# Last self attention of a two-layer Perceiver: division after the product, one subtraction on GpSimd, the row sums of W behind the output projection

## The chip, the cores and the metric

The kernel runs on one core of a Trainium2 chip. The metric is the device time of one execution in microseconds (us), as the median of several runs; lower is better. Engines are named as in the profile: PE is TensorE (PEld its weight loads), DVE VectorE, ACT ScalarE, POOL GpSimd, SP the engine that issues the DMAs. All data is 32-bit floating point.

## The reference

128 latent rows of width 256 (`x`) pass through two layers against one context of 12544 rows of width 192. Each layer is a cross attention to the context, a self attention over the 128 rows, and a mixture of 8 experts of which each row uses 2; each of the six steps reads a layer-normalised `x` and is added to `x`. The change lies in the second layer's self attention, and in one product that it needs from W:

```python
def _L1_attn_ref(x, W):                       # x: layer-normalised, [1, 128, 256]
    scale = 1.0 / sqrt(D)                     # D = 256
    scores = einsum('btd,bsd->bts', x, x) * scale
    probs = softmax(scores, axis=-1)
    vacuum_mask = probs < 0.01
    vacuum_energy = where(vacuum_mask, probs, 0.0)
    vac_sum = vacuum_energy.sum(axis=-1, keepdims=True)
    vac_in = broadcast_to(vac_sum, (B, T, D))
    casimir = einsum('btd,od->bto', vac_in, W)
    sparse_probs = where(vacuum_mask, 0.0, probs)
    sparse_probs = sparse_probs / (sparse_probs.sum(axis=-1, keepdims=True) + 1e-09)
    attended = einsum('bts,bsd->btd', sparse_probs, x)
    return attended + casimir * 0.01
```

Since `vac_in` is one number per row, `casimir` is that number times the row sums of W.

## The kernel before

The 128 latents lie on the 128 partitions throughout; `x` is one tile of 128 x 256, and every step makes a new one. The two cross attentions take most of the time.

**Cross attention of the second layer.** 16 heads of width 64 are taken in pairs, eight passes (`PASSES`) of 13 periods (`NS`) over 1024 context rows each, 104 periods (`NP`) in all. A loop over `t` runs the scores of period `t` and, `LAG` = 14 periods later, the product with the values, so its last 14 rounds hold the values and products of the last pass alone. Each such round has TensorE compute the values of one period (L228, L235), ScalarE copy them out of PSUM (L962) and exponentiate a probability tile (L1057), and TensorE multiply the two into the PSUM tile `both` (L1069). VectorE and GpSimd subtract the row maximum (L1051) ahead of that, and VectorE adds up the exponentials (L1092). In the round `t == NP + 3` two products stand that belong to no period: the row sums of W, as a product of a tile of ones with the transposed W (`awT`), into the second half of `both`'s second bank (L1160), and the output projection of the first seven passes (L1138). After the loop come the last denominator (L1124, L1133), the last pass's projection (L1138), the bias row (`add_row`, L126) and the residual `x4` (L162).

**Self attention.** `layernorm` (statistics on VectorE, a square root on ScalarE, L146 on VectorE, two transposes on TensorE at L156 and their copy at L157), then the scores (L1248), their maximum, the exponential on ScalarE (L1254), the sum, the reciprocal and the probabilities `a1_p` (L1261). From there VectorE makes the small probabilities, their sum, the large ones, their sum and its reciprocal, divides, TensorE transposes (L156), VectorE copies (L157), TensorE multiplies with the normalised `x` (L1278), and VectorE adds the residual and the row sums of W times the small probabilities' sum (L1283).

**Experts of the second layer.** `layernorm`, the router's product (L1291), then for each expert 32 products of 128 x 128 into PSUM (L1302), a gate on ScalarE, a multiplication on VectorE (L1313), and four products back to width 256 (L1340). Their weights, 24 transfers of 512 KB, are issued by SP in the order of the program, each as soon as its slot of the ring of 28 tiles is free; the same slots hold the probability tiles of the cross attention.

**What sets the order.** The code around the change stands under a manual schedule: each engine executes its instructions in the order of the program, and waits on semaphores between engines are put in by the framework. PSUM tiles of 512 elements (`ps_mm`, `ps_t`, `ps_w` are one kind) come from a pool of four buffers. [...]In the profile's names leading letters of a tile are cut (`a1_p` is `a_p`), and `xn` of the self attention is `ln` on its own or `ln4`.

Of the kernel before, what the change touches and what calls it, by code (L numbers as in the profile page):

```python
# [8 lines left out]
F32 = mybir.dt.float32  # L9
AF = mybir.ActivationFunctionType  # L10
ALU = mybir.AluOpType
AX = mybir.AxisListType

P = 128
D = 256
# [18 lines left out]
def perceiver(ctx: ExitStack, tc: tile.TileContext, a: dict, out: bass.AP):  # L34
    nc = tc.nc
# [31 lines left out]
    ps_wide, ps_t, ps_mm = ps_s, ps_w, ps_w  # L67
# [81 lines left out]
    def transposed(pool, t, n, name, tag, bank=None, **kw):  # L149

        tT = pool.tile([P, n, P], F32, tag=tag, name=name, **kw)
        for g in range(0, n, 4):
            m = min(4, n - g)
            pt = ps_t(f"{name}_ps{g}") if bank is None else bank
            for i in range(m):
                nc.tensor.transpose(pt[:, i * P : (i + 1) * P], t[:, (g + i) * P : (g + i + 1) * P], ident)  # L156
            nc.vector.tensor_copy(tT[:, g : g + m, :].rearrange("p c n -> p (c n)"), pt[:, : m * P])  # L157
        return tT
# [736 lines left out]
    with tc.tile_pool(name="l1x", bufs=1) as work:  # L895
# [246 lines left out]
        with tc.manual_schedule():  # L1142
            for t in range(NP + LAG):
                before, live = t - LAG, t < NP
                e = before + 1
                end = live and periods[t][1] == NS - 1
                if before == NP - 1:
                    pass_end(PASSES - 1)
                o = attend(before) if 0 <= before else None
                if 0 < t <= NP and periods[t - 1][1] == NS - 1:  # L1150
                    pass_spread(periods[t - 1][0])
                if t == NP + 1:
                    context(t)
                    ywo.extend(
                        slot_weight(f"ywo{i}", a["L1_xattn_Wo"][512 * i : 512 * i + 512]) for i in range(2)
                    )
                if t == NP + 3:

                    for c in range(2):
                        nc.tensor.matmul(  # L1160
                            final["both"][:, 1, D : 2 * D], ones, awT[:, c, :], start=(c == 0), stop=(c == 1)
                        )
                    projected(0, PASSES - 1)
                if t != NP + 1 and (NS <= t + 1 < NP or 0 <= e + 1 < NP):
                    context(t)
                k = keys(t + 1) if NS <= t + 1 < NP else None
                if t < NS:
                    kTs[t] = firstk[t]
                v = values(e + 1) if 0 <= e + 1 < NP else None
                sts = scores(t) if live else None  # L1170
                if v:
                    if k:
                        k[0]()
                    v[0]()
                if 0 <= e < NP and periods[e][1] == 0:
                    shifted(e)
                if 0 <= e + 1 < NP and periods[e + 1][1]:
                    shifted(e + 1)
                late = 0 <= e < NP and periods[e][1] < 2
                if 0 <= e < NP and not late:  # L1180
                    exponents(e)
                    if e == NP - 1:
                        table(AF.Sqrt, "ln4_table0")
                if o is not None:
                    added(before, 0)
                    if not end:
                        added(before, 1)
                    attended(before, o)

                short = k and v and periods[t + 1][1] == NS - 1  # L1190

                def evicted():
                    k[2](1)
                    for r in range(2):
                        v[2](r)

                if short:
                    for f in (k, v):
                        for r in range(2):
                            f[1](r)  # L1200
                if live:
                    keep(t, sts, evicted if short else None)
                if t < NS:
                    fill(2 if t < 4 else 1)
                if t in (5, 7):
                    queries(*((1, 5) if t == 5 else (5, 8)))
                if end:
                    fold(periods[t][0])
                if late:
                    exponents(e)  # L1210
                if short:
                    k[2](0)
                elif k and v:
                    for r in range(2):
                        k[1](r)
                    for r in range(2):
                        k[2](r)
                final_v = v and t == NP - 1
                if final_v:
                    for f in v[1:]:  # L1220
                        for r in range(2):
                            f(r)
                if end:
                    pass_maximum(periods[t][0])
                if o is not None:
                    if end:
                        added(before, 1)
                    del ps[before]
                if v and not short and not final_v:
                    for r in range(2):  # L1230
                        v[1](r)
                    for r in range(2):
                        v[2](r)
                if 0 < before and periods[before - 1][1] == NS - 1:
                    pass_end(periods[before - 1][0])
            nc.vector.tensor_tensor(oT[:, PASSES - 1, :], final["both"][:, 0, 0:P], os[PASSES - 1], ALU.mult)
            projected(PASSES - 1, PASSES)
            py = final["both"][:, 1]
            add_row(py[:, :D], ROW_BO, D)
            x = residual(x, py[:, :D], "x4")  # L1240
            wsum = final["both"][:, 1, D : 2 * D]


    with tc.tile_pool(name="l1a", bufs=1) as work, tc.manual_schedule():
        xn, xnT = layernorm(x, "ln4")
        ps = ps_mm("a1_ps")
        for c in range(2):
            nc.tensor.matmul(ps[:, :P], xnT[:, c, :], xnT[:, c, :], start=(c == 0), stop=(c == 1))  # L1248
        nmax = small.tile([P, 1], F32, tag="s_nmax", name="a1_nmax")
        nc.vector.tensor_reduce(nmax, ps[:, :P], AX.X, ALU.max, negate=True)  # L1250
        nb = small.tile([P, 1], F32, tag="s_nb", name="a1_nb")
        nc.vector.tensor_scalar(nb, nmax, 1.0 / 16.0, None, ALU.mult)
        ex = work.tile([P, P], F32, name="a1_e")
        nc.scalar.activation(ex, ps[:, :P], AF.Exp, bias=nb, scale=1.0 / 16.0)  # L1254
        table(AF.Sqrt, "ln5_table0")
        tot = small.tile([P, 1], F32, tag="s_tot", name="a1_tot")
        nc.vector.tensor_reduce(tot, ex, AX.X, ALU.add)
        rtot = small.tile([P, 1], F32, tag="s_rtot", name="a1_rtot")
        nc.vector.reciprocal(rtot, tot)
        pr = work.tile([P, P], F32, name="a1_p")  # L1260
        nc.vector.tensor_scalar(pr, ex, rtot, None, ALU.mult)  # L1261
        vac = work.tile([P, P], F32, name="a1_vac")
        nc.vector.scalar_tensor_tensor(vac, pr, 0.01, pr, ALU.is_lt, ALU.mult)
        vs = small.tile([P, 1], F32, tag="s_vs", name="a1_vs")
        nc.vector.tensor_reduce(vs, vac, AX.X, ALU.add)
        sp = work.tile([P, P], F32, name="a1_sp")
        nc.vector.tensor_tensor(sp, pr, vac, ALU.subtract)
        ss = small.tile([P, 1], F32, tag="s_ss", name="a1_ss")
        nc.vector.tensor_reduce(ss, sp, AX.X, ALU.add)
        ss1 = small.tile([P, 1], F32, tag="s_ss1", name="a1_ss1")  # L1270
        nc.vector.tensor_scalar(ss1, ss, 1e-9, None, ALU.add)
        rs = small.tile([P, 1], F32, tag="s_rs", name="a1_rs")
        nc.vector.reciprocal(rs, ss1)
        spn = work.tile([P, P], F32, name="a1_spn")
        nc.vector.tensor_scalar(spn, sp, rs, None, ALU.mult)
        spT = transposed(work, spn, 1, "a1_spT", tag="spT")
        pa = ps_mm("a1_pa")
        nc.tensor.matmul(pa[:, :D], spT[:, 0, :], xn, start=True, stop=True)  # L1278
        x = residual(x, pa[:, :D], "x5a")
        vs1 = small.tile([P, 1], F32, tag="s_vs1", name="a1_vs1")  # L1280
        nc.vector.tensor_scalar(vs1, vs, 0.01, None, ALU.mult)
        y = xp.tile([P, D], F32, tag="x", name="x5")
        nc.vector.scalar_tensor_tensor(y, wsum, vs1, x, ALU.mult, ALU.add)  # L1283
        x = y


    with tc.tile_pool(name="l1f", bufs=2) as work, tc.manual_schedule():
# [108 lines left out]
```

## Time and profile before

| | |
|---|---|
| median of 3 runs | 1573.84 us (1573.14 to 1574.27) |
| the profiled execution | 1575.52 us |
| its span, first to last instruction | 1573.8 us |
| PE busy | 1498.2 us, 95% |
| DVE busy | 1153.5 us, 73% |
| ACT busy | 997.9 us, 63% |
| POOL busy | 873.4 us, 55% |
| mean granted TensorE clock | 0.991 |
| chain that ended last, by engine | PE 65%, DVE 7%, ACT 4% |
| row sums of W (L1160) | 1459.6 to 1460.6 us |
| end of the cross attention, last residual | about 1511 us |
| self attention, layer norm included | about 1511 to 1522.3 us |
| router and experts | about 1522.3 us to the end |

A row of a timeline has the start in us from the span's start, the duration in us, the engine, the line, the operation, what it writes `<-` what it reads, the sizes, and the number of instructions merged; in brackets stands how long the engine was idle before and what ended that. A row of a table of stretches has the busy time in us and the number of instructions of PE, PEld, DVE, ACT and POOL, then the granted TensorE clock as a share of full speed, the share of time in which the DMA engines were busy, and GB/s. A 32-bit matrix product appears as two records per instruction.

### The profile page before, as it was taken

Reading aid. Unit: us, or ns where it says so; the run is one execution under the profiler, and the core shown is the slowest. Engines: PE = TensorE matmul, PEld = TensorE weight load, DVE = VectorE, ACT = ScalarE, POOL = GpSimd, SP = SyncE. Lnnn points to the kernel's source line nnn. Section 1 sums busy time; section 2 is a strip of 40 time slices with the busy share of each in tenths; the row PEclk is TensorE's granted clock in tenths of the full one; section 3 lists DMA queues with packets and bytes.
Section 4 is the critical chain, followed back from the end, with each engine's and each line's share of the span. In section 5 each row is a group of like instructions: output and inputs, shape, how many; then the busy total and the mean of one; then the engine's idle time right before and its main releaser. Section 6 shows DMA issues by size and latency. Waiting matters only on the chain.

```text
span 1573.8 us, 39767 instructions
## 1 busy us (share of the span) xinstructions
PE 1498.2 (95%) x17138; PEld 1151.3 (73%) x17138; DVE 1153.5 (73%) x1219; ACT 997.9 (63%) x1233; POOL 873.4 (55%) x570
## 2 busy tenths in 40 slices
PE   7999989999879999999999999999999999999979
PEld 4666656666545877787787787787787787788968
DVE  3899887999884337777777777777777777778742
ACT  4898988999883235665565565565565665666541
POOL 0488877988840000864864864864764764764400
PEclk9999999999999999999999999999999999999979
DMA  3111021211086861222222222232232232234680
GB/s 105 44 60 42 27 62 42 62 42 42 14 246 189 264 168 29 82 82 86 82 83 85 81 86 82 81 93 75 84 97 70 86 95 73 90 88 131 176 293 4
DMA packets 68737, 146.62 MB, mean 93 GB/s; under 512 B 8905, under 2 KB 27089, under 8 KB 68562
## 3 DMA queue, kind: packets, MB, share of 16 engines
q1 hardware_dynamic: 68258, 143.30, 30.7%
q8 instruction: 135, 2.21, 0.6%
q10 hardware_dynamic: 304, 0.79, 0.2%
q14 instruction: 40, 0.33, 0.1%
HBM read 143.92 MB, written 0.13 MB: 92 GB/s over the span
## 4 chain that ended last, share of the span: by engine, by line
PE 65%; DVE 7%; ACT 4%; issue 1%; DMA 1%; POOL 1%; DVEq 0%; ACTq 0%
PE x_s L977 11%; PE x_v L235 11%; PE x_k L213 10%; PE x_o L1069 10%; PE x_v L228 6%; PE x_k L210 4%; PE f_h L1302 2%; PE f_h L839 2%; PE f_py L856 2%; DVE x_part L1096 2%; PE x_both L1069 1%; ACT x_p L522 1%; PE k L213 1%; DVE x_folded L1024 1%; POOL x_p L511 1%
## 5 line engine op out<-in xcount | busy, mean ns | idle before, releaser
L1051 POOL TENSOR_TENSOR x_p<-x_p,x_spread 128x1024 f32<-128x1024 f32 (+1 forms) x186 | 427.5, 2325 | 151.4 <-ACT x_spread L1042 151.1
L511 POOL TENSOR_TENSOR x_p<-x_p,x_spread 128x512 f32<-128x512 f32 (+1 forms) x184 | 324.4, 1809 | 127.1 <-ACT x_spread L499 65.3
L1096 DVE TENSOR_REDUCE x_part<-x_p 128x256 f32<-128x1024 f32 (+1 forms) x175 | 329.6, 1923 | 0.0
L994 ACT COPY x_p<-x_s 128x1024 f32<-128x1024 f32 (+1 forms) x200 | 197.9, 996 | 179.4 <-DVE x_mx L1001 97.6
L1001 DVE TENSOR_TENSOR x_mx<-x_s,x_mx 128x1024 f32<-128x1024 f32 (+1 forms) x161 | 193.4, 1201 | 128.7 <-PE x_s L977 120.2
L1101 POOL TENSOR_TENSOR x_sums<-x_sums,x_part 128x256 f32<-128x256 f32 x161 | 117.6, 731 | 299.8 <-DVE x_part L1096 297.9
L446 ACT COPY x_p<-x_s 128x1024 f32<-128x1024 f32 x196 | 193.3, 1015 | 50.8 <-PE x_s L433 35.5
L235 PEld LDWEIGHTS x_v<-ywv_lo,x_ctx_lo 128*128 128x128 f32 x1568 | 189.3, 192 | 38.4 <-issue 36.8
L1057 ACT ACTIVATE x_p<-x_p 128x1024 f32<-128x1024 f32 (+1 forms) x200 | 197.9, 1037 | 2.2 <-DVE x_p L1051 2.0
L522 ACT ACTIVATE x_p<-x_p 128x1024 f32<-128x1024 f32 x196 | 196.5, 1063 | 0.2 <-DVE x_p L511 0.2
L235 PE MATMUL x_v<-ywv_lo,x_ctx_lo 128*128 128x128 f32 x1568 | 193.2, 276 | 0.0
L452 DVE TENSOR_TENSOR x_mx<-x_s,x_mx 128x1024 f32<-128x1024 f32 x140 | 168.1, 1220 | 32.7 <-PE x_s L433 17.8
L977 PE MATMUL x_s<-x_qT,x_kT 64*128 64x128 f32 x2744 | 177.7, 279 | 0.0
L977 PEld LDWEIGHTS x_s<-x_qT,x_kT 64*128 64x128 f32 x2744 | 160.2, 188 | 15.6 <-issue 15.4
L213 PE MATMUL x_k<-x_ctx_lo,ywk_lo 128*128 128x512 f32 (+1 forms) x364 | 171.6, 594 | 0.0
L1069 PE MATMUL x_o<-x_p,x_v 128*64 128x128 f32 x2744 | 169.6, 276 | 0.4
L962 ACT COPY x_v<-x_v 128x512 f32<-128x512 f32 (+1 forms) x208 | 116.4, 563 | 77.2 <-PE x_v L235 76.5
L1069 PEld LDWEIGHTS x_o<-x_p,x_v 128*64 128x64 f32 x2744 | 148.4, 137 | 11.0 <-issue 1.7
L228 PEld LDWEIGHTS x_v<-ywv_hi,x_ctx_hi 64*128 64x128 f32 x1568 | 105.5, 188 | 46.7 <-issue 25.4
L433 PE MATMUL x_s<-x_qz,x_kT 32*128 32x256 f32 x1568 | 118.6, 403 | 17.7 <-ACT x_p L446 16.6
L535 PE MATMUL x_o<-x_p,x_v 128*32 128x128 f32 x3136 | 113.0, 278 | 10.4 <-ACT x_p L522 7.6
L535 PEld LDWEIGHTS x_o<-x_p,x_v 128*32 128x32 f32 x3136 | 82.8, 111 | 54.5 <-ACT x_p L522 18.2
(268 smaller groups left out, 1774.0 us busy)
## 6 DMA issues: line engine op xcount, KB each, us to landing
x_ctx_lo<-in_ctxT_dram SPq DMA_DIRECT2D x119, 512.0 KB, 4.1
x_ctx_hi<-in_ctxT_dram SPq DMA_DIRECT2D x238, 128.0 KB, 4.0
f_w<-in_L_ffn_W_dram SPq DMA_DIRECT2D x32, 512.0 KB, 4.9
k_lo<-in_ctxT_dram SPq DMA_DIRECT2D x12, 512.0 KB, 8.3
f_gating<-n_kernel_gating_EDF_dram SPq DMA_DIRECT2D x8, 512.0 KB, 10.6
f_up<-L_ffn_kernel_up_EDF_dram SPq DMA_DIRECT2D x8, 512.0 KB, 10.4
f_wd<-ffn_kernel_down_EFD_dram SPq DMA_DIRECT2D x8, 512.0 KB, 10.3
k_hi<-in_ctxT_dram SPq DMA_DIRECT2D x24, 128.0 KB, 7.6
```

Source lines behind the costliest of these rows:

```text
L213: nc.tensor.matmul(ps[r][:, :h], wk[0][:, js], lo[:, r * h : (r + 1) * h], start=False, stop=True)
L228: nc.tensor.matmul(ps[r][:, ks], hi[rs, ks], wv[1][rs, js], start=(kc == 0), stop=False, skip_group_check=True,)
L235: nc.tensor.matmul(ps[r][:, kc * P : (kc + 1) * P], lo[:, r * h + kc * P : r * h + (kc + 1) * P], wv[0][:, js], start=False, stop=True, sk ...
L511: engine.tensor_tensor(v, v, by[:, banks].unsqueeze(2).to_broadcast([P, n, 2, 256]), ALU.add)
L522: nc.scalar.activation(ps[t][k], ps[t][k], AF.Exp)
L535: nc.tensor.matmul(os[b][32 * i : 32 * i + 32, u * P : (u + 1) * P], v[:, 2 * g + c, 17 * (2 * i + u) : 17 * (2 * i + u) + 32], p[i // 2][ ...
L977: nc.tensor.matmul(st[:, u, c * P : (c + 1) * P], kTs[t][rs, ks], qT[rs, j, :], start=True, stop=True)
L994: nc.scalar.copy(scores_kept(ps[t][i], sts[i].shape[2] // P), sts[i])
L1051: engine.tensor_tensor(v, v, by.unsqueeze(2).to_broadcast([P, 2, n, P]), ALU.add)
L1057: nc.scalar.activation(v, v, AF.Exp)
L1069: nc.tensor.matmul(o[us, 0:P], vs[t][:, c0 + c, us], p[:, n0 : n0 + P], start=(c0 + c == 0 and (s == 0 or not whole)), stop=(c0 + c == tot ...
L1096: nc.vector.tensor_reduce(part, v, AX.X, ALU.add)
```

## The change

- The row sums of W (two products of 128 x 256) leave the round `t == NP + 3`. They now stand after the residual `x4` in the program, behind the bias row in TensorE's order, with a PSUM tile of their own (`a1_pc`).
- The large probabilities are made straight from the probabilities, by one instruction with the comparison turned round, and not by subtraction.
- Their transpose follows at once, without the division; the sum, the guard and the reciprocal stand between the transpose and its copy in VectorE's order. The transpose is written out in place of the helper.
- The small probabilities are now the difference of the two, computed on GpSimd after the product with `xn` is issued; VectorE sums them after the copy.
- The residual takes the row sums' term first (L1281 of the changed kernel), then the product times the reciprocal (L1283), both as one multiply-and-add instruction. Formerly it was one addition and one multiply-and-add.

VectorE has two instructions less, GpSimd one more, TensorE as many as before.

```diff
                 if t == NP + 3:
-                    for c in range(2):
-                        nc.tensor.matmul(
-                            final["both"][:, 1, D : 2 * D], ones, awT[:, c, :], start=(c == 0), stop=(c == 1)
-                        )
                     projected(0, PASSES - 1)
...
             x = residual(x, py[:, :D], "x4")
-            wsum = final["both"][:, 1, D : 2 * D]
+            pc = ps_mm("a1_pc")
+            for c in range(2):
+                nc.tensor.matmul(pc[:, :D], ones, awT[:, c, :], start=(c == 0), stop=(c == 1))
...
         nc.vector.tensor_scalar(pr, ex, rtot, None, ALU.mult)
-        vac = work.tile([P, P], F32, name="a1_vac")
-        nc.vector.scalar_tensor_tensor(vac, pr, 0.01, pr, ALU.is_lt, ALU.mult)
-        vs = small.tile([P, 1], F32, tag="s_vs", name="a1_vs")
-        nc.vector.tensor_reduce(vs, vac, AX.X, ALU.add)
         sp = work.tile([P, P], F32, name="a1_sp")
-        nc.vector.tensor_tensor(sp, pr, vac, ALU.subtract)
+        nc.vector.scalar_tensor_tensor(sp, pr, 0.01, pr, ALU.is_ge, ALU.mult)
+        pt = ps_t("a1_spT_ps")
+        nc.tensor.transpose(pt[:, 0:P], sp, ident)
         ss = small.tile([P, 1], F32, tag="s_ss", name="a1_ss")
         nc.vector.tensor_reduce(ss, sp, AX.X, ALU.add)
         ss1 = small.tile([P, 1], F32, tag="s_ss1", name="a1_ss1")
         nc.vector.tensor_scalar(ss1, ss, 1e-9, None, ALU.add)
         rs = small.tile([P, 1], F32, tag="s_rs", name="a1_rs")
         nc.vector.reciprocal(rs, ss1)
-        spn = work.tile([P, P], F32, name="a1_spn")
-        nc.vector.tensor_scalar(spn, sp, rs, None, ALU.mult)
-        spT = transposed(work, spn, 1, "a1_spT", tag="spT")
+        spT = work.tile([P, P], F32, name="a1_spT")
+        nc.vector.tensor_copy(spT, pt[:, 0:P])
         pa = ps_mm("a1_pa")
-        nc.tensor.matmul(pa[:, :D], spT[:, 0, :], xn, start=True, stop=True)
-        x = residual(x, pa[:, :D], "x5a")
+        nc.tensor.matmul(pa[:, :D], spT, xn, start=True, stop=True)
+        vac = work.tile([P, P], F32, name="a1_vac")
+        nc.gpsimd.tensor_tensor(vac, pr, sp, ALU.subtract)
+        vs = small.tile([P, 1], F32, tag="s_vs", name="a1_vs")
+        nc.vector.tensor_reduce(vs, vac, AX.X, ALU.add)
         vs1 = small.tile([P, 1], F32, tag="s_vs1", name="a1_vs1")
         nc.vector.tensor_scalar(vs1, vs, 0.01, None, ALU.mult)
-        y = xp.tile([P, D], F32, tag="x", name="x5")
-        nc.vector.scalar_tensor_tensor(y, wsum, vs1, x, ALU.mult, ALU.add)
-        x = y
+        y = xp.tile([P, D], F32, tag="x", name="x5a")
+        nc.vector.scalar_tensor_tensor(y, pc[:, :D], vs1, x, ALU.mult, ALU.add)
+        x = xp.tile([P, D], F32, tag="x", name="x5")
+        nc.vector.scalar_tensor_tensor(x, pa[:, :D], rs, y, ALU.mult, ALU.add)
```

## The prediction, made before the changed kernel ran

> **What bounds the kernel now.** I read the page's slices first. TensorE is nearly full everywhere except in the last slices but one, and there its granted clock falls:
>
> ```profile
> PE   7999989999879999999999999999999999999979
> PEclk9999999999999999999999999999999999999979
> ```
>
> The chain of waits is 65% TensorE. In order of time it lies on TensorE alone up to 1507.9 us and again from 1525.4 us. The change touches both sides of that first border. So the second view is TensorE's timeline around 1460 us, where the row-sum product stands (L1160):
>
> ```profile
> 1457.72 1.97 PE L1069 MATMUL x_both<-x_p,x_v 128*64 128x128 f32 x32
> 1459.62 1.13 PE L1160 MATMUL x_both<-awT,ones 128*128 128x256 f32 x4
> 1460.58 3.19 PE L1138 MATMUL x_both<-ywo,x_oT 128*128 128x256 f32 x14
> ```
>
> No idle time stands before these groups, and the waits of TensorE between 1458 and 1510 us hold one entry, 1.0 us before the last projection. The four records of L1160 are paid in full.
>
> The third view is VectorE's timeline through the attention (start, duration, in brackets the idle time before):
>
> ```profile
> 1516.91 0.29 DVE L1261 TENSOR_SCALAR a_p<-a_e,a_rtot 128x128 f32<-128x128 f32 x1
> 1517.23 0.29 DVE L1263 SCALAR_TENSOR_TENSOR a_vac<-a_p 128x128 f32<-128x128 f32 x1
> 1517.56 0.29 DVE L1265 TENSOR_REDUCE a_vs<-a_vac 128x1 f32<-128x128 f32 x1
> 1517.76 0.28 DVE L1267 TENSOR_TENSOR a_sp<-a_p,a_vac 128x128 f32<-128x128 f32 x1
> 1518.08 0.29 DVE L1269 TENSOR_REDUCE a_ss<-a_sp 128x1 f32<-128x128 f32 x1
> 1518.40 0.15 DVE L1271 TENSOR_SCALAR a_ss<-a_ss 128x1 f32<-128x1 f32 x1
> 1518.58 0.16 DVE L1273 RECIPROCAL a_rs<-a_ss 128x1 f32<-128x1 f32 x1
> 1518.78 0.28 DVE L1275 TENSOR_SCALAR a_spn<-a_sp,a_rs 128x128 f32<-128x128 f32 x1
> 1519.70 0.29 DVE L157 COPY a_spT<-a_spT_ps 128x128 f32<-128x128 f32 x1 [0.63 <-PE a_spT_ps L156]
> 1521.30 0.42 DVE L162 TENSOR_TENSOR x5a<-a_pa,x 128x256 f32<-128x256 f32 x1 [1.31 <-PE a_pa L1278]
> 1521.64 0.14 DVE L1281 TENSOR_SCALAR a_vs<-a_vs 128x1 f32<-128x1 f32 x1
> 1521.83 0.48 DVE L1283 SCALAR_TENSOR_TENSOR x<-x_both,a_vs,x5a 128x256 f32<-128x256 f32 x1
> ```
>
> Everything here is serial: TensorE waits for VectorE and the reverse, and nothing else fills the time. What this chain loses, the end gains. The chain puts 8.5 us before L1257 down to a weight DMA (f_up). I don't believe it: that transfer belongs to the expert layer, behind this layer in the program, and ScalarE's a_e ended 0.09 us before L1257 began.
>
> The fourth view is a table of stretches, cut at the steps of the granted clock (PE busy is the second number, the clock the third from the right):
>
> ```profile
> 1505.90:1509.31 3.41, 2.39 (x45) 2.15 (x41) 1.25 (x2) 1.03 (x2) 0.00 (x0) 1.00 1.06 372
> 1509.31:1512.72 3.41, 1.27 (x4) 0.54 (x4) 1.61 (x5) 0.94 (x2) 0.00 (x0) 1.00 1.06 377
> 1512.72:1516.14 3.42, 1.89 (x6) 1.22 (x6) 0.87 (x3) 1.05 (x3) 0.00 (x0) 0.50 1.06 373
> ```
>
> The clock halves at 1512.72 and is whole again at 1529.79, five stretches of 3.41 us later.
>
> **Part 1: the row sums leave the full stage.** L1160 starts at 1459.62 and L1138 at 1460.58: at most 0.96 us. From 1459.62 to the next group (L228 at 1463.70) 18 records take 4.08 us, 0.227 each, so four are 0.91; four weight loads alone (0.19 each) give 0.76. I take 0.91, with 0.76 and 0.96 as ends. It reaches the end if nothing else is late in that stage. ScalarE idles 1.65 us per period there waiting for x_v of TensorE itself; GpSimd's last spread ends at 1472.4, for tiles used later; the context loads are issued several periods ahead of use and land in about 4 us; the last sums (x_allsums, ends 1505.80) are 0.5 us ahead of x_den, and follow TensorE through ScalarE. SP's expert loads follow the freed slots and move with it; the last lands near 1526, the first expert needs its own, issued at 1490, only after 1522. None is next.
>
> **Part 2: the row sums behind the projection.** The same two products (four records) now stand behind add_row (L126, last starts at 1510.2, done 1510.6) and ahead of the transposes of ln4 (1512.85), which wait for VectorE, ScalarE and VectorE. At 0.227 each they need 0.91 us, at half clock, as a_pa (1.22 for two records), 2.4 us at most; the gap is 2.27. So 0, at worst 0.2. The residual x4 waits for add_row alone.
>
> **Part 3: a shorter chain.** Before, from a_vac's start (1517.23) to the start of the last x (1521.83) it is 4.60 us. After:
> - a_sp is one instruction of a_vac's form, from a_p: 0.29. As from a_spn's start to its transpose (1518.78 to 1519.22), 0.44; I take 0.45.
> - transpose start to copy start 0.48 (1519.22 to 1519.70), copy to a_pa 0.35 (1520.05), a_pa to the next VectorE start 1.25 (1521.30).
> - Sum 2.53, so the last x starts at 1519.76, and lasts 0.48 as before: 2.07 us saved.
>
> The sum over a_sp, the guard and the reciprocal (a_ss, ss1, rs) take the 0.62 us in which VectorE formerly idled for the transpose: rs starts at 1518.06, and the copy's turn is 1518.16, just when its transpose is ready. Worth 0 (up to 0.1 late).
>
> **Part 4: GpSimd's subtraction.** a_vac moves to GpSimd, which has nothing behind it, but VectorE's reduction a_vs waits for it, and behind that in VectorE's queue are vs1, x5a and the last x. Its price: GpSimd's forms are 2367 ns at 1024 elements, 1271 at 512, 731 at 256, about 2.1 ns an element over 0.19 us, so an estimate of 0.46 us at 128. In the timeline GpSimd starts 0.14 us after VectorE's x_part (1444.27 to 1444.41). Its instruction carries twelve waits; ScalarE's a_e, with eleven, began 0.16 us after VectorE instead of the usual 0.04, so 0.12 more. a_sp ends at 1517.52, a_vac at 1518.24, ahead of VectorE's turn after the copy (1518.36). Then a_vs 0.33, vs1 0.18, x5a 0.50 with their gaps: done 1519.37, 0.39 before a_pa is ready. Cost 0; if it came later than 0.4 us, each further us costs one. Not below 0, for nothing waits for it earlier.
>
> [...]By the rows this operation has run hundreds of times in the program, and starts 0.14 us after its releaser even after 5 us of idleness, though here it has idled 45 us.[...]
>
> **Part 5: the clock.** [...]In the table above the window before the drop was 37% busy, not idle; elsewhere one of 64% busy (430.71 to 434.12) kept its clock. [...]With this run's grid, the transposes of ln4 move 0.91 us forward into the full-clock window: 0.44 (x_mt, L246) instead of 0.66, 0.22 gained. Then f_pl starts 3.2 us earlier, at 1522.2, and the next full busy window ends at 1526.38, so 4.2 us of TensorE work at half clock instead of 4.4: 0.1. On another grid a_ps too runs at full clock (another 0.6), or the warm-up falls a window later (up to 1.2 lost). I take 0.25.
>
> **Sum.** 0.91 + 0 + 2.07 + 0 + 0.25 = 3.23 us. The profiled execution took 1575.5 us for a span of 1573.8, and would take 1572.3. It lies 1.7 us above the median of the runs; the difference carries over: 1573.84 - 3.23 = 1570.6.
>
> **Rivals.**
> - The row sums' 0.91 us is taken by another wait in the full stage (x_v copies, context loads): 1571.5. Against it: no such idle time in TensorE's rows.
> - GpSimd is late by more than its slack without a stall (rows of GpSimd are rough, and twelve waits were never seen on it), by 0.5 to 1.5 us: 1571.1 to 1572.1. For it: a cross-engine trip on a path with 0.4 us of slack.
> [...]- The transpose is moved but the chain isn't cut, since the copy waits for VectorE's three small steps or the product for a PSUM bank: at most 0.6 us lost, 1571.2. Against it: the product waits only for the copy.
>
> **Chances.** A difference of 0.2% (3.15 us, below 1570.7 or above 1577.0) is about what a measurement of this kernel can tell. As summed, 1569.4 to 1571.6 by the grid: 0.72, of which 0.49 below 1570.7. Another wait takes the row sums: 0.11 (0.02 below, by the grid). GpSimd late by up to 1.5: 0.10. The 6 us: 0.03, of which 0.02 beyond 1577. Chain not cut: 0.04 (0.01 below). Faster 0.52, within 0.46, slower 0.02. The range runs from the lower end of the grid, 1569.4, to the late GpSimd, 1572.3; it leaves out the 6 us and the tails.
>
> **What would show it.** L1138's first record 0.9 us earlier against L1069; L1238 beside ln4's VectorE and ScalarE rows, and ln4's transposes not waiting for it; a_vac on GpSimd at about 0.5 us, ending before VectorE has copied a_spT; a_pa the last to end before the final x, which starts 2.5 us after a_sp. I am wrong if VectorE's a_vs waits on GpSimd for more than 0.4 us, if the stage before 1508 us keeps its length, or if the number of half-clock windows grows.

## The result, and the profile after

The changed kernel took 1571.74 us (median of 22 runs, 1567.77 to 1577.54); the kernel before, on the same chip, 1575.46 (22 runs, 1570.39 to 1580.95). The ratio is 0.9975, interval 0.9965 to 0.9986: 3.9 us less, between 2.2 and 5.5. The three runs from which the prediction started (1573.84) lie 1.6 us below the median of all 22. The profiled execution took 1571.92 us for a span of 1570.2; before, 1575.52 for 1573.8, so 3.6 us less.

First the two rows of slices of the page after:

```profile
PE   7999989999879999999999999999999999999979
PEclk9999999999989999999999999999999999999989
```

The tail looks much the same: one slice with idle time and a lowered clock. The digit 8 in the twelfth slice of PEclk is new and lies far ahead of the change. Ahead of the tail, windows at half clock begin at 15.0, 233.5, 424.6, 431.5, 438.3, 455.4 and 622.6 us after, and at 236.2, 437.5 and 468.3 us before. Up to the row sums' round (1457.72 us before, 1457.10 after) this pair differs by 0.62 us, although both kernels have the same instructions up to there. Over all twelve profiles of this document that round starts anywhere between 1454.7 and 1462.2 us, so the 0.62 us is not counted as the change's; where it comes from was not looked for.

TensorE's timeline around the place where the row sums stood:

```profile
1457.10 1.97 PE L1069 MATMUL x_both<-x_p,x_v 128*64 128x128 f32 x32
1459.00 3.29 PE L1138 MATMUL x_both<-ywo,x_oT 128*128 128x256 f32 x14
1462.22 1.16 PE L228 MATMUL x_v<-ywv_hi,x_ctx_hi 64*128 64x128 f32 x16
```

L1138 now follows L1069 directly. From the start of L1069 to that of L228 it is 5.12 us. Before, L228 began 5.98 us behind L1069's 1457.72:

```profile
1463.70 0.38 PE L228 MATMUL x_v<-ywv_hi,x_ctx_hi 64*128 64x128 f32 x2
```

That is 0.86 less. The later stage, up to the start of x_rden, keeps its 44.15 us, so nothing else became late there.

VectorE's timeline through the attention (start, duration, in brackets the idle time before and its releaser):

```profile
1514.90 0.29 DVE L1261 SCALAR_TENSOR_TENSOR a_sp<-a_p 128x128 f32<-128x128 f32 x1
1515.22 0.29 DVE L1265 TENSOR_REDUCE a_ss<-a_sp 128x1 f32<-128x128 f32 x1
1515.54 0.15 DVE L1267 TENSOR_SCALAR a_ss<-a_ss 128x1 f32<-128x1 f32 x1
1515.73 0.17 DVE L1269 RECIPROCAL a_rs<-a_ss 128x1 f32<-128x1 f32 x1
1515.82 0.29 DVE L1271 COPY a_spT<-a_spT_ps 128x128 f32<-128x128 f32 x1
1516.03 0.28 DVE L1277 TENSOR_REDUCE a_vs<-a_vac 128x1 f32<-128x128 f32 x1
1516.33 0.15 DVE L1279 TENSOR_SCALAR a_vs<-a_vs 128x1 f32<-128x1 f32 x1
1516.52 0.48 DVE L1281 SCALAR_TENSOR_TENSOR x5a<-a_pc,a_vs,x 128x256 f32<-128x256 f32 x1
1517.42 0.48 DVE L1283 SCALAR_TENSOR_TENSOR x<-a_pa,a_rs,x5a 128x256 f32<-128x256 f32 x1 [0.42 <-PE a_pa L1273]
```

The three small steps (the sum a_ss, its guard, the reciprocal a_rs) stand where VectorE used to wait for the transpose. The last x is the only row with idle time, and that ends with a_pa. From the start of a_sp to the start of the last x it is 2.52 us; before it was 4.60 from a_vac. GpSimd's timeline holds one row:

```profile
1515.49 0.45 POOL L1275 TENSOR_TENSOR a_vac<-a_p,a_sp 128x128 f32<-128x128 f32 x1 [43.23 <-ACT ln_table L132]
```

It had idled 43 us, began 0.30 us after a_sp's end (1515.19), and was done at 1515.94, before a_vs began at 1516.03.

TensorE beside it:

```profile
1509.04 1.13 PE L1238 MATMUL a_pc<-awT,ones 128*128 128x256 f32 x4
1511.27 0.44 PE L156 MATMUL ln4T_ps<-ident,ln 128*128 128x128 f32 x2 [1.11 <-DVE ln L146]
1512.23 0.71 PE L1245 MATMUL a_ps<-ln4T 128*128 128x128 f32 x4 [0.52 <-DVE ln4T L157]
1515.33 0.45 PE L1263 MATMUL a_spT_ps<-ident,a_sp 128*128 128x128 f32 x1 [2.39 <-DVE a_sp L1261]
1516.16 1.22 PE L1273 MATMUL a_pa<-ln,a_spT 128*128 128x256 f32 x2 [0.38 <-DVE a_spT L1271]
...
1520.88 1.02 PE L1290 MATMUL f_pl<-wr,ln5T 128*128 128x8 f32 x4 [0.52 <-DVE ln5T L157]
```

The row sums (L1238) end 1.1 us before the transposes of ln4, which wait for VectorE. Those transposes and the scores a_ps ran at full clock here (0.44 and 0.71). Before, they ran at half clock:

```profile
1512.85 0.66 PE L156 MATMUL ln4T_ps<-ident,ln 128*128 128x128 f32 x2 [2.27 <-DVE ln L146]
1514.03 1.22 PE L1248 MATMUL a_ps<-ln4T 128*128 128x128 f32 x4 [0.52 <-DVE ln4T L157]
...
1525.38 0.99 PE L1291 MATMUL f_pl<-wr,ln5T 128*128 128x8 f32 x4 [0.61 <-DVE ln5T L157]
```

But after the change f_pl began at 1520.88, and the clock was whole again only at 1527.15. The table of stretches, cut at the clock's steps (PE busy is the second number, the clock the third from the right), has this:

```profile
1510.08:1513.49 3.41, 1.24 (x7) 0.72 (x6) 1.61 (x6) 1.78 (x3) 0.00 (x0) 1.00 1.07 372
1513.49:1516.91 3.42, 1.19 (x3) 0.68 (x3) 2.58 (x11) 1.85 (x3) 0.45 (x1) 0.50 1.07 371
1516.91:1520.32 3.41, 1.09 (x4) 0.29 (x2) 1.77 (x6) 1.67 (x3) 0.00 (x0) 0.50 1.07 372
1520.32:1523.73 3.41, 2.89 (x14) 2.85 (x14) 1.70 (x8) 0.38 (x2) 0.00 (x0) 0.50 1.06 374
1523.73:1527.15 3.42, 3.42 (x18) 3.42 (x17) 2.09 (x12) 1.69 (x3) 0.00 (x0) 0.50 0.24 78
1527.15:1530.56 3.41, 3.41 (x33) 3.41 (x32) 0.69 (x1) 0.60 (x1) 0.00 (x0) 1.00 0.00 0
```

The half clock holds for four stretches instead of five, but more of the experts' work falls into them. From the start of f_pl to the full clock it is 6.27 us (1520.88 to 1527.15); before it was 4.41 (1525.38 to 1529.79), as the table of before ends so:

```profile
1526.38:1529.79 3.41, 3.41 (x17) 3.41 (x18) 2.51 (x14) 0.39 (x2) 0.00 (x0) 0.50 0.10 31
1529.79:1533.21 3.42, 3.42 (x32) 3.42 (x32) 1.53 (x6) 2.17 (x4) 0.00 (x0) 1.00 0.00 0
```

The experiments are read by the same stretches of the tail, each between the starts of two rows of a profile, in us. "Final x" is the experts' last sum; "filled" kernels have products in TensorE's waits that nobody reads:

| kernel | L1069 to L228 | x4 to a_tot | chain (a_vac or a_sp to last x) | f_pl to final x | L1069 to final x | half-clock windows |
|---|---|---|---|---|---|---|
| before | 5.98 | 5.77 | 4.60 | 45.23 | 112.89 | 5 |
| after | 5.12 | 4.92 | 2.52 | 46.13 | 109.91 | 4 |
| row sums back | 5.98 | 5.48 | 2.53 | 45.19 | 110.50 | 4 |
| a_vac on VectorE | 5.12 | 4.94 | 2.54 | 45.91 | 109.73 | 4 |
| four a_vac | 5.12 | 5.06 | 3.78 | 45.06 | 110.24 | 4 |
| division before | 5.11 | 5.45 | 3.56 | 46.39 | 111.68 | 5 |
| TensorE filled | 5.12 | 4.91 | 2.19 | 43.15 | 106.36 | 0 |
| changed, again | 5.12 | 5.06 | 2.54 | 45.65 | 109.60 | 4 |
| row sums alone | 5.11 | 5.43 | 4.60 | 45.87 | 112.24 | 5 |
| filled more | 5.12 | 4.94 | 2.19 | 43.15 | 106.37 | 0 |
| filled, a_vac on VectorE | 5.12 | 4.92 | 2.52 | 43.15 | 106.68 | 0 |
| before, filled | 5.98 | 5.00 | 3.92 | 44.75 | 110.73 | 1 |

The stretches left out (L228 to x_rden, x_rden to x4, a_tot to a_sp, last x to f_pl) differ by 0.02 us or less, except the last one: 3.55 where the row sums stand at their old place, 3.46 where they are moved, 3.40 with the plain final sum, 3.2 to 3.3 at full clock.

Two of these differences are no matter of the clock. Where the row sums stand at their old place (before, row sums back, before filled), ln4's transposes start 0.56 us after the start of ln's row (L146) and f_pl 0.57 after that of ln5's copy, at half and at full clock; in the nine other profiles it is 0.47 and 0.48. In those three traces TensorE waits for two semaphores ahead of each of the two, in the others for one. A likely reason, not tested, is that a_pc takes one more of the four PSUM buffers, so that these products get buffers with another last reader. So moving the row sums saves 0.09 us twice, beside the 0.86.

### The profile page after: what moved, and what is told of

Its sections match the earlier page's. It is cut to its first block, busy times and chain, and to the rows that moved or that the text cites. A ratio compares the mean times of both kernels' runs of the same rounds, so it can differ in the third digit from the quotient of the medians.

```text
span 1570.2 us, 39771 instructions
## 1 busy us (share of the span) xinstructions
PE 1499.2 (95%) x17138; PEld 1154.7 (74%) x17138; DVE 1152.8 (73%) x1217; ACT 998.3 (64%) x1233; POOL 874.1 (56%) x571
## 4 chain that ended last, share of the span: by engine, by line
PE 65%; DVE 7%; ACT 4%; issue 1%; POOL 1%; DMA 1%; SPq 0%; DVEq 0%; ACTq 0%
PE x_v L235 11%; PE x_s L977 11%; PE x_k L213 10%; PE x_o L1069 10%; PE x_v L228 6%; PE x_k L210 4%; PE f_h L1301 2%; PE f_h L839 2%; PE f_py L856 2%; DVE x_part L1096 2%; PE x_both L1069 1%; ACT x_p L522 1%; PE k L213 1%; DVE x_mx L452 1%; DVE x_folded L1024 1%
## 5 line engine op out<-in xcount | busy, mean ns | idle before, releaser
L1069 PE MATMUL x_o<-x_p,x_v 128*64 128x128 f32 x2744 | 169.6, 276 | 0.4
L1069 PEld LDWEIGHTS x_o<-x_p,x_v 128*64 128x64 f32 x2744 | 148.4, 137 | 11.0 <-issue 1.7
L228 PEld LDWEIGHTS x_v<-ywv_hi,x_ctx_hi 64*128 64x128 f32 x1568 | 105.4, 188 | 46.3 <-issue 25.0
```

The costliest lines, as they stand in the source:

```text
L228: nc.tensor.matmul(ps[r][:, ks], hi[rs, ks], wv[1][rs, js], start=(kc == 0), stop=False, skip_group_check=True,)
L1069: nc.tensor.matmul(o[us, 0:P], vs[t][:, c0 + c, us], p[:, n0 : n0 + P], start=(c0 + c == 0 and (s == 0 or not whole)), stop=(c0 + c == tot ...
```

## The experiments

The theory: 0.9 us come from the emptied place in the full stage (the cross attention's rounds, in which TensorE has no idle time), 2.1 from the chain, nothing from GpSimd, and the clock gives or takes up to a microsecond by where its windows fall. The rivals: GpSimd sets the end; the division is not what shortens the chain; the gain comes from the clock.

**The row sums put back.** The changed kernel, with the product again in the full stage:

```
                 if t == NP + 3:
+                    for c in range(2):
+                        nc.tensor.matmul(
+                            final["both"][:, 1, D : 2 * D], ones, awT[:, c, :], start=(c == 0), stop=(c == 1)
+                        )
...
-            pc = ps_mm("a1_pc")
-            for c in range(2):
-                nc.tensor.matmul(pc[:, :D], ones, awT[:, c, :], start=(c == 0), stop=(c == 1))
+            wsum = final["both"][:, 1, D : 2 * D]
...
-        nc.vector.scalar_tensor_tensor(y, pc[:, :D], vs1, x, ALU.mult, ALU.add)
+        nc.vector.scalar_tensor_tensor(y, wsum, vs1, x, ALU.mult, ALU.add)
```

> The changed kernel with the row sums of W back in the round of the cross attention, all else as changed. My theory (the row sums are paid in full there): from the product with the values (L1069) to the next values (L228) around that round 5.98 us as in the kernel before, not 5.12 as in the changed one; the attention chain from a_sp to the last x stays 2.52; so 0.9 us slower than the changed kernel, and the half clock begins earlier, so that ln4's transposes or the scores run at half clock in more executions (up to 0.8 more). Rival (the row sums were hidden, or the stage fills up with another wait): the stretch L1069 to L228 stays at 5.1, or the stage up to the last denominator is as long as in the changed kernel.

1573.81 us (22 runs), ratio to before 0.9984 (0.9976 to 0.9992). TensorE's timeline of this kernel:

```profile
1459.32 1.97 PE L1069 MATMUL x_both<-x_p,x_v 128*64 128x128 f32 x32
1461.22 1.13 PE L1159 MATMUL x_both<-awT,ones 128*128 128x256 f32 x4
1462.19 3.19 PE L1138 MATMUL x_both<-ywo,x_oT 128*128 128x256 f32 x14
1465.30 0.94 PE L228 MATMUL x_v<-ywv_hi,x_ctx_hi 64*128 64x128 f32 x12
```

The 5.98 us are back and the chain is 2.53: the two parts are independent, and the row sums' place in the full stage costs 0.86.

**The small probabilities on VectorE.** The changed kernel, with one word different:

```
-        nc.gpsimd.tensor_tensor(vac, pr, sp, ALU.subtract)
+        nc.vector.tensor_tensor(vac, pr, sp, ALU.subtract)
```

> The changed kernel with the one subtraction back on VectorE, in the same place. My theory (there is 0.4 us of slack before the product is ready): VectorE needs 0.3 us more between the copy and x5a, x5a ends about 0.1 us before the product, so a_sp to the last x stays at 2.5 us (at most 2.6) and the time is that of the changed kernel. Rival (GpSimd is what frees VectorE): a_sp to the last x grows by the 0.3 us of the subtraction.

1571.03 us (22 runs), ratio 0.9971 (0.9962 to 0.9980), beside 0.9975 of the changed kernel. VectorE's timeline:

```profile
1513.44 0.29 DVE L1271 COPY a_spT<-a_spT_ps 128x128 f32<-128x128 f32 x1
1513.65 0.28 DVE L1275 TENSOR_TENSOR a_vac<-a_p,a_sp 128x128 f32<-128x128 f32 x1
...
1514.47 0.48 DVE L1281 SCALAR_TENSOR_TENSOR x5a<-a_pc,a_vs,x 128x256 f32<-128x256 f32 x1
1515.06 0.48 DVE L1283 SCALAR_TENSOR_TENSOR x<-a_pa,a_rs,x5a 128x256 f32<-128x256 f32 x1
```

The last x has no bracket any more: the subtraction fills the 0.42 us in which VectorE waited for a_pa, and the chain is 2.54. Moving it to GpSimd was worth 0.02 us here.

**Four subtractions on GpSimd.** Three of them repeat the same result:

```
-        nc.gpsimd.tensor_tensor(vac, pr, sp, ALU.subtract)
+        for _ in range(4):
+            nc.gpsimd.tensor_tensor(vac, pr, sp, ALU.subtract)
```

> The changed kernel with the same subtraction four times in a row on GpSimd, so that the small probabilities come about 1.4 us later. My theory: 0.45 us of that is slack (0.09 before VectorE's turn, 0.40 before the product), so a_sp to the last x grows from 2.52 to about 3.5 us, and the waits show VectorE's a_vs on GpSimd for 1.3 us. Rival (slack is larger, since the residual could use what is there): no growth; rival (GpSimd's rows are rough and its real end is later): growth by the full 1.4 us.

1573.92 us (18 runs), ratio 0.9989 (0.9980 to 0.9999). GpSimd's timeline, and then VectorE's:

```profile
1517.54 2.05 POOL L1276 TENSOR_TENSOR a_vac<-a_p,a_sp 128x128 f32<-128x128 f32 x4 [43.69 <-ACT ln_table L132]
```

```profile
1519.62 0.29 DVE L1278 TENSOR_REDUCE a_vs<-a_vac 128x1 f32<-128x128 f32 x1 [1.46 <-POOL a_vac L1276]
...
1520.72 0.48 DVE L1284 SCALAR_TENSOR_TENSOR x<-a_pa,a_rs,x5a 128x256 f32<-128x256 f32 x1
```

Now a_vs waits for GpSimd. Four take 2.05 us, 1.60 more than one, and the chain grows by 1.26, so 0.34 us of them were covered. The end of the chain does follow GpSimd as soon as its slack is used up. That 3.78 came instead of about 3.5 has two parts: the three further ones took 0.53 each and not 0.46 (1.60 for 1.4), and the slack was 0.34 and not 0.45.

**The division before the transpose again.** The changed kernel with spn put back, and a plain sum at the end:

```
-        pt = ps_t("a1_spT_ps")
-        nc.tensor.transpose(pt[:, 0:P], sp, ident)
...
+        spn = work.tile([P, P], F32, name="a1_spn")
+        nc.vector.tensor_scalar(spn, sp, rs, None, ALU.mult)
+        pt = ps_t("a1_spT_ps")
+        nc.tensor.transpose(pt[:, 0:P], spn, ident)
...
-        nc.vector.scalar_tensor_tensor(x, pa[:, :D], rs, y, ALU.mult, ALU.add)
+        nc.vector.tensor_tensor(x, pa[:, :D], y, ALU.add)
```

> The changed kernel with the division back ahead of the transpose; the large probabilities still come straight from the probabilities, and the subtraction stays on GpSimd. My theory: sum, guard, reciprocal and division (0.32 + 0.18 + 0.20 + 0.32) come back onto the chain, a_sp to the last x is 2.52 + 1.0 = 3.5 us; of the 2.08 us that the chain lost, 1.0 is the division and 1.06 the small probabilities and the residual. Rival (the gain is in the order of VectorE's queue alone): 2.8 us or less, or 4.2 or more.

1573.04 us (20 runs), ratio 0.9987 (0.9977 to 0.9997). The chain is 3.56: taking the division off the path, and with it the sum, the guard and the reciprocal that it waits for, gives 1.04 of the 2.08 us. No run isolates the other 1.04, but the rows of before have it: 0.53 from a_vac to a_sp (1517.23 to 1517.76), now that a_sp comes straight from a_p, and 0.53 from x5a to the last x (1521.30 to 1521.83), now that x5a is done before a_pa.

**The row sums alone.** The kernel before, with only the product moved behind the projection (wsum is then the first 256 columns of its own tile, x4 and the chain as before):

> The kernel before with the row sums of W moved behind the output projection and nothing else. My theory: L1069 to L228 5.1 us instead of 5.98, the attention chain (a_vac to the last x) still 4.60 us, half clock begins later so that ln4's transposes run at full clock; 0.9 us faster by the row sums and 0.2 to 0.8 by the clock in front, less what the clock gives back at the experts: about 1.2 us (0.9992). Rival (the clock is the larger part of the change): 2 us or more; rival (the gain comes with the shorter chain alone): none.

1574.53 us (14 runs), ratio 0.9995 (0.9982 to 1.0008). By its profile the full stage is 0.87 us shorter and the chain unchanged at 4.60. The whole tail is only 0.65 shorter (112.89 to 112.24), half of what was expected, since the experts lost 0.64 to the clock. The time alone can't tell this from no change.

**The changed kernel once more**, for how far one profile differs from the next:

> The changed kernel again, as a yardstick for the other runs of this call: 0.9975 of the time before, within its interval; from L1069 to L228 around the last big projection 5.1 us, a_sp to the last x 2.52 us; the place of the half clock differs by execution.

1572.47 us (12 runs), ratio 0.9984 (0.9971 to 0.9997). The chain is 2.54 and the full stage 5.12, as before; x4 to a_tot is 0.14 us longer and f_pl to the final x 0.48 shorter. Here the clock was whole 5.28 us behind the start of f_pl (1521.93 to 1527.21, four windows of 3.41 us behind a drop just ahead of 1513.60) and not 6.27, and half of that difference is 0.50.

**TensorE kept busy.** The changed kernel, with products in the waits whose results nobody reads:

```
+            def fill_pe(n):
+                for _ in range(n):
+                    nc.tensor.matmul(final["both"][:, 0, :D], ones, awT[:, 0, :], start=True, stop=True)
+
+            fill_pe(1)
...
+        fill_pe(4)
...
+        fill_pe(4)
```

The first stands behind the row sums, the others behind the scores and behind a_pa.

> The changed kernel with products that nobody reads (tile of ones with the transposed W, 256 wide, 0.45 us each at full clock) in TensorE's waits of the last self attention: one after the row sums, four after the scores, four after the product. The output is unaffected. My theory (the tail's half clock is set by TensorE's idle windows, and costs half of f_pl, of the first experts' products and of four small products): no half-clock window from the last projection on, a_pa to the last x start 0.7 instead of 1.25 us, f_pl to the last x 43 instead of 45 to 46 us; 3 to 4 us faster than the changed kernel. Rival (the filling is in the way: it is still running when the next product is ready, or the clock halves all the same): no gain, and ln5's or a_sp's transposes wait for TensorE itself.

1569.12 us (13 runs), ratio 0.9963 (0.9953 to 0.9973). TensorE's timeline:

```profile
1512.37 0.44 PE L156 MATMUL ln4T_ps<-ident,ln 128*128 128x128 f32 x2 [0.68 <-DVE ln L146]
1513.33 0.71 PE L1251 MATMUL a_ps<-ln4T 128*128 128x128 f32 x4 [0.52 <-DVE ln4T L157]
1513.87 1.89 PE L1242 MATMUL x_both<-awT,ones 128*128 128x256 f32 x8
1516.43 0.30 PE L1270 MATMUL a_spT_ps<-ident,a_sp 128*128 128x128 f32 x1 [0.67 <-DVE a_sp L1268]
1517.23 0.70 PE L1280 MATMUL a_pa<-ln,a_spT 128*128 128x256 f32 x2 [0.50 <-DVE a_spT L1278]
1517.77 1.89 PE L1242 MATMUL x_both<-awT,ones 128*128 128x256 f32 x8
...
1521.86 2.03 PE L1309 MATMUL f_h<-ln5T,f_gating 128*128 128x128 f32 x16
```

The fillers (L1242) end before what follows them; TensorE still waits for VectorE. All is at full clock: a_pa 0.70 instead of 1.22, the first sixteen f_h 2.03 instead of 3.76. From f_pl to the end it is 43.15 us. The whole tail is 3.55 us shorter than that of the changed kernel. The time is clearly below that of before, and 3.35 us below that of the changed kernel run again on the same chip (1572.47; ratio 0.9984, and the two intervals just touch). In the chain VectorE is now last:

```profile
1518.18 0.48 DVE L1291 SCALAR_TENSOR_TENSOR x<-a_pa,a_rs,x5a 128x256 f32<-128x256 f32 x1
```

The last x follows x5a (1517.60 to 1518.08) with no idle time in brackets, so a_pa is no longer what ends last.

**More of the fillers**, 2, 5 and 5 instead of 1, 4 and 4:

> As the kernel with the filling products, with two, five and five of them (0.91, 2.3 and 2.3 us), which fills the waits nearly to the brim. If the share of busy time in a window decides the clock, it holds the clock at least as surely as one, four and four: as fast, within 0.5 us, and more even. Rival (there is no slack left): the last one is still running when ln4's, a_sp's or ln5's transpose is ready, 0.2 to 1 us slower than with one, four and four.

1569.04 us (7 runs), ratio 0.9960 (0.9946 to 0.9975); the tail is the same within 0.01 us. With no half-clock window left in either tail, nothing more is to be had from the clock there.

**Filled, and a_vac on VectorE:**

> The changed kernel with the filling products (one, four, four) and with the subtraction on VectorE. At half clock VectorE had 0.4 us of slack before the product; at full clock the product is 0.5 us sooner, and VectorE ends last. My theory: here GpSimd is worth its 0.3 us: a_sp to the last x 2.5 us instead of 2.19, L1069 to the end 106.7 instead of 106.36. Rival (VectorE has slack at full clock too): 2.2 us.

The chain is 2.52 instead of 2.19. So with the clock held, GpSimd's part in the change is worth 0.33 us, where at half clock it was worth 0.02. The time, 1567.15 us, comes from six runs; its ratio of 0.9949 (0.9930 to 0.9968) is lower than that of the filled kernel, not higher, and overlaps it, so the 0.33 us rests on the profile alone.

**The kernel before, filled**, with 3, 7 and 5 products behind the bias row, the scores and a_pa:

> The kernel before with the same filling products in its longer waits (three after the bias row, seven after the scores, five after the product; into the PSUM tile of the sums, which nobody reads any more). With the clock held in both, the difference to the changed kernel with filling products is what the change itself saves. My theory: no half-clock window in the tail, L1069 to L228 5.98, a_vac to the last x 3.95 us (4.60 less 0.15 and 0.5 for the faster transpose and product), f_pl to the end 43.15; from L1069 to the end 109.0, 2.6 us more than 106.36. Rival (a good part of what the change saves is the clock): 1.5 us more or less.

1570.60 us (11 runs), ratio 0.9968 (0.9956 to 0.9980). No half-clock window was expected, but one was left in the profiled execution, from 1523.4, and made f_pl to the end 1.60 us longer than in the filled changed kernel. The rest of the tail differs between the two by 110.73 - 106.36 - 1.60 = 2.77 us: 0.86 in the full stage, 1.73 in the chain (3.92 to 2.19), and the 0.09 us twice, ahead of ln4's transposes and of f_pl. That is the change with the clock held. It is less than at half clock because the full clock shortens the old chain by 0.68 (4.60 to 3.92) and the new one only by 0.33 (2.52 to 2.19), where VectorE then ends last.

The times don't bear this 2.77 out by themselves. The two filled kernels ran on different chips, and their ratios, 0.9968 and 0.9963, can't be told apart. On the same chip as the filled kernel before ran the changed one with a_vac on VectorE: 3.45 us less (1567.15 to 1570.60), for tails that differ by 4.05; with six and eleven runs that fits, but does not prove it. And the old kernel with fillers alone (0.9968) is no slower than the changed kernel without them (0.9975 and 0.9984): by these times, holding the clock is worth about as much as the change.

## Why the prediction was right

**Part 1** said 0.91; it is 0.86, and 0.86 comes back when it is undone. **Part 2** said 0: the row sums end 1.1 us before ln4's transposes can start, so their new place costs nothing. What it did not see is that the move also saves 0.09 us twice. **Part 3** said 2.07, from 4.60 to 2.53; it is 2.08, to 2.52. The three steps do lie in VectorE's former wait, and the copy started 0.49 us after the transpose, against 0.48 before, so it lost nothing to them. The division is half of this gain, as its undoing shows.

**Part 4** said that a_vac takes 0.46 and begins 0.26 after a_sp; it took 0.45 and began after 0.30. The slack of 0.39 to 0.4 was measured as 0.34 with four subtractions. No run shows the 6 us that stands among the chances: after 43 to 45 us of idleness a_vac began 0.30 to 0.32 us after a_sp's end, in the changed kernel and its repeat, with the row sums back, with four subtractions and with the division before. What the prediction did not ask is whether this part was needed. At half clock it was not: on VectorE the subtraction fits into the same slack (a chain of 2.54 beside 2.52).

**Part 5**, the clock, is the term that was mis-sized. In front, x4 to a_tot shrank by 0.85; 0.09 of that is the semaphore wait, and about 0.75 the clock, against 0.22 in the sum, since a_ps too was at full clock. The back lost 0.90 instead of gaining 0.1: f_pl came 4.5 us earlier but the full clock only 2.64, so 6.27 us of TensorE's work ran at half clock, and not 4.2. Both departures stand in the prediction as what another grid of windows might do (0.6 more, up to 1.2 lost); it had summed with the grid of one execution. Net the clock is about -0.15, against a gain of 0.25. That the two nearly cancel is luck, and differs by execution: the changed kernel's front was 4.92 and 5.06 in two profiles, its back 46.13 and 45.65.

In the sum, the four parts without the clock were put at 2.98 us; the profiles have 0.86 + 2.08 + 0.18 = 3.12, and with the clock 2.98 for the whole tail (112.89 to 109.91). The stretch ahead of the change makes the rest of the pair's 3.6. The times put the saving at 3.9 us, and their interval (2.2 to 5.5) holds both 2.98 and the predicted 3.23, so they can't say which is nearer. The predicted 1570.6 stands 1.1 us under the measured 1571.74 because its three runs of before were low by 1.6, while the predicted saving was 0.5 us below the 3.7 between the medians; the two errors partly cancelled. Of the rivals, none happened: the full stage took back nothing, GpSimd was not late, the copy did not wait.

## What to carry to other kernels

A serial stretch shortens by what leaves its longest path, so follow the starts on the engine that waits: the division could move behind the product because a scale of each row passes through it, and the small steps fit where VectorE had to wait anyway. Before moving an operation to another engine, ask how long the waiting engine is idle afterwards; here 0.42 us of idleness already held it. And where TensorE has many short waits, look at its clock: products that nobody reads, placed in those waits, shortened this tail by 3.55 us in the profiles, more than the change itself once the clock is held (2.77).

## What the runs showed of the hardware

The half-clock spans in the tails are whole multiples of 3.41 us (17.07 before, 13.65 after). The window just ahead of the drop was not idle: TensorE was 37% busy in it before, and 36% after. While the clock was down, a window 85% busy (1520.32 to 1523.73, after) was followed by another at half clock; elsewhere one 91% busy (437.53 to 440.94, before) was followed by full clock, as the 100% busy ones at the ends of these tails were. The busy share alone does not decide. In the kernel before a window 73% busy (464.84 to 468.26) stood right ahead of one at half clock, and one 64% busy (430.71 to 434.12) was followed by full clock. And in the kernel before with fillers two windows in a row were equally busy, and the clock fell behind the second:

```profile
1516.58:1519.99 3.41, 2.10 (x9) 1.75 (x10) 1.96 (x9) 0.00 (x0) 0.00 (x0) 1.00 1.06 375
1519.99:1523.40 3.41, 2.11 (x13) 1.45 (x13) 1.62 (x6) 1.78 (x3) 0.00 (x0) 1.00 1.07 376
1523.40:1526.81 3.41, 3.41 (x18) 3.41 (x18) 2.49 (x14) 0.43 (x2) 0.00 (x0) 0.50 0.49 164
```

Both are 62% busy. No run here settles what decides the clock. That one, four and four fillers left the changed kernel's tail without a half-clock window is shown; how few would do was not tried, and in the old kernel three, seven and five left one.

One more wait on a semaphore went with a later start: with two ahead of it f_pl started 0.57 us after the start of the copy that it needs, with one 0.48, in all twelve profiles. GpSimd's a_vac, which carries twelve waits, began 0.30 us after a_sp's end, where a sum of GpSimd in the cross attention began 0.14 us after VectorE (1444.27 to 1444.41, before); whether that is the waits or the long idleness was not tested.
